# Layer 0's first loads as ordered 256 KB pieces, and VectorE's ids from an on-chip row

## The chip, the core and the metric

The kernel runs on one core of a Trainium2 chip. A core has several engines, each with its own in-order instruction queue: TensorE (PE) multiplies matrices, VectorE (DVE) and ScalarE (ACT) work on rows, GpSimd (POOL) does the same and issues gathers, and SyncE (SP) issues most of the DMA transfers. Sixteen DMA engines move data between DRAM and the on-chip memory of 128 partitions. Products are accumulated in a second on-chip memory, PSUM. The metric is the device time of one launch in microseconds, as the median of several runs.

## What is computed

The input `x` has 64 sequences of 32 positions of 512 numbers. Four residual layers follow one another. Only the first is touched here:

```python
# layer 0: conditioning, then a feed-forward block
w = weight[adapter_ids]                       # 8 sets of 512x512, one chosen per sequence
y = einsum('bsi,boi->bso', x, w)
logits = y @ gate_w                           # 8 experts, top 2
routing, _ = top_k(logits, 2)
h = relu(y @ up_w) ** 2                       # 512 -> 1024
shared = h @ down_w                           # 1024 -> 512
moe = ((y @ fc1_w) @ expert_w) * sum(routing)
routed = moe @ fc2_w
x = x + layernorm(shared + routed) * gamma + beta
```

The ids lie between 3 and 7. Layer 1 is another conditioned feed-forward block, layer 2 is attention over a paged cache with a feed-forward block behind it, and layer 3 is a small last one. All data are float32.

## The kernel before

The 2048 rows of `x` are 16 tiles of 128 rows. A tile holds four sequences (`SEQ = 4`). Layer 0 (`layer0`) works on groups of `G = 4` tiles, so there are four groups, each with 16 sequences and so 16 ids. `KC = 4` is the number of 128-row slices of the inner dimension of 512.

The loads come first, all of them issued by SyncE in the order in which the code names them: the group's transposed input `xT` (1 MB, line 85, which is the line of the helper `load`), the eight `sets` of conditioning weights as one transfer of 2 MB for each slice k (line 159), then `fc1T`, `expert`, the gate columns of `latent`, `up` (2 MB), `down` (2 MB), `fc2`, `gamma` and `beta`.

`products(g, xT)` is a generator which computes y for a group. It first fills 16 VectorE registers with the group's ids (line 171). The source is a row in DRAM:

```python
_, ids = nc.values_load_multi_w_load_instructions(
    a["ids0"][0:1, SEQ * G * g:SEQ * G * (g + 1)], engines=[mybir.EngineType.DVE],
    min_val=0, max_val=n_sets - 1)
```

Then, for each slice k and each tile t, VectorE copies the four chosen 128x512 weight slices, found by register, into a tile `w` (line 179; three such buffers), and TensorE multiplies each sequence's 32 rows by its own slice (line 183), accumulating in PSUM (`py`). That is 64 copies a group. After the last slice each `py` is copied out by VectorE (`y`, line 189), and transposed by TensorE (line 117) with ScalarE copying the result to `yT` (line 118).

For group 0 the generator is run to its end. Then `fc1T` and `expert` are multiplied into `latent` (the product is called `pfe`, line 122). The main loop over groups computes the eight blocks of `h` (`ph`, line 122; relu on ScalarE, line 210; the square as `hT` on VectorE, line 211), and takes two steps of the next group's generator after each block. Then, tile by tile, it computes the routed part (`pl`; `top`, line 221; `routed_by`, line 223; `routed`, line 225), the product with `down` (`pd`, line 228), the transposes of `routed`, the product with `fc2` (line 232) and the normalisation (lines 234 to 245). The last part of the generator (the y copies and transposes of the next group) is taken inside the first tile.

The order on each queue isn't the order of the code: a scheduler places an instruction as soon as it takes its operands to be ready. Nothing in the program before ties a group's register loads to any other work. `tc.issue_after(ins)` is the program's way of saying that what is traced inside it stands behind `ins` on the same engine's queue.

Of the kernel before, what the change touches and what calls it, by code (L numbers as in the profile page):

```python
# [24 lines left out]
F32 = mybir.dt.float32  # L25
I32 = mybir.dt.int32
# [7 lines left out]
P = 128  # L34
B, S, D = 64, 32, 512
NT = B * S // P
SEQ = P // S
KC = D // P
# [90 lines left out]
def layer0(c, x_in, x_out):  # L129

    tc, nc, a = c.tc, c.nc, c.a
    INT, LAT, NE = 1024, 256, 8
    G = 4
    N = G * P
    n_sets = a["cond0T"].shape[0]
    with ExitStack() as ctx:

        fp = ctx.enter_context(tc.tile_pool(name="l0_first", bufs=1))
        sp = ctx.enter_context(tc.tile_pool(name="l0_seq_weights", bufs=3))
        tx = ctx.enter_context(tc.tile_pool(name="l0_transposed_x", bufs=2))
        up_p = ctx.enter_context(tc.tile_pool(name="l0_up", bufs=1))
        wp = ctx.enter_context(tc.tile_pool(name="l0_weights", bufs=1))
        xp = ctx.enter_context(tc.tile_pool(name="l0_x", bufs=2))
        gp = ctx.enter_context(tc.tile_pool(name="l0_group", bufs=2))
        tp = ctx.enter_context(tc.tile_pool(name="l0_tile", bufs=2))
        ps = ctx.enter_context(tc.tile_pool(name="l0_psum", bufs=2, space=PSUM))

        def transposed_x(g):
            return c.load(tx, "xT", [P, KC, N],
                          a["xT"][:, g * N:(g + 1) * N].rearrange("(k p) n -> p k n", p=P))

        xT = transposed_x(0)

        sets = fp.tile([P, KC, n_sets, D], F32, name="sets")
        for k in range(KC):
            nc.sync.dma_start(sets[:, k], a["cond0T"][:, k * P:(k + 1) * P, :].rearrange("e p o -> p e o"))
        fc1T = c.chunks(fp, "fc1T_0")  # L160
        expert = c.chunks(fp, "expert0")
        latent = wp.tile([P, KC, LAT + NE], F32, name="latent")
        nc.sync.dma_start(latent[:, :, LAT:], a["gate0"].rearrange("(k p) n -> p k n", p=P))
        up = c.chunks(up_p, "up0")
        down = c.chunks(wp, "down0")
        fc2 = c.chunks(wp, "fc2_0")
        gamma, beta = c.row(wp, "gamma0"), c.row(wp, "beta0")

        def products(g, xT):

            _, ids = nc.values_load_multi_w_load_instructions(
                a["ids0"][0:1, SEQ * G * g:SEQ * G * (g + 1)], engines=[mybir.EngineType.DVE],
                min_val=0, max_val=n_sets - 1)
            pys = [ps.tile([P, D], F32, tag=f"y{t}", bufs=1, name="py") for t in range(G)]
            for k in range(KC):
                for t in range(G):
                    w = sp.tile([P, SEQ, D], F32, name="w")
                    for j in range(SEQ):
                        nc.vector.tensor_copy(w[:, j, :], sets[:, k, ds(ids[SEQ * t + j], 1), :]
                                              .rearrange("p a o -> p (a o)"))  # L180
                    for j in range(SEQ):
                        q = slice(S * j, S * j + S)
                        nc.tensor.matmul(pys[t][q, :], xT[:, k, t * P + S * j:t * P + S * j + S],  # L183
                                         w[:, j, :], start=k == 0, stop=k == KC - 1)
                    yield
            yT = gp.tile([P, KC, N], F32, name="yT")
            for t in range(G):
                y = tp.tile([P, D], F32, name="y")
                nc.vector.tensor_copy(y, pys[t])
                c.transposed(ps, "tr", y, yT[:, :, t * P:(t + 1) * P])  # L190
            yield yT

        steps = products(0, xT)
        for yT in steps:
            pass
        for m in range(KC):
            pl = ps.tile([P, LAT], F32, tag="tr", name="pfe")
            c.accumulate(pl, [(fc1T[:, k, m * P:(m + 1) * P], expert[:, k, :]) for k in range(LAT // P)])
            nc.scalar.copy(latent[:, m, :LAT], pl)

        for g in range(NT // G):
            more = iter(())
            if g + 1 < NT // G:
                more = products(g + 1, transposed_x(g + 1))
            hT = gp.tile([P, INT // P, N], F32, name="hT", bufs=1)
            for f in range(INT // P):
                ph = ps.tile([P, N], F32, tag="mm", name="ph")
                c.accumulate(ph, [(up[:, k, f * P:(f + 1) * P], yT[:, k, :]) for k in range(KC)])
                r = tp.tile([P, N], F32, name="relu")
                nc.scalar.activation(r, ph, AF.Relu)  # L210
                nc.vector.tensor_tensor(hT[:, f, :], r, ph, ALU.mult)
                for _ in range(2):
                    next(more, None)
            for t in range(G):
                T = G * g + t
                q = slice(t * P, (t + 1) * P)
                xt = c.load(xp, "xt", [P, D], x_in(T))
                pl = ps.tile([P, LAT + NE], F32, tag="tr", name="pl")
                c.accumulate(pl, [(yT[:, k, q], latent[:, k, :]) for k in range(KC)])
                top = tp.tile([P, 8], F32, name="top")  # L220
                nc.vector.max(top, pl[:, LAT:])
                r = tp.tile([P, 1], F32, name="routed_by")
                nc.vector.tensor_tensor(r, top[:, 0:1], top[:, 1:2], ALU.add)
                routed = tp.tile([P, LAT], F32, name="routed")
                nc.scalar.activation(routed, pl[:, :LAT], AF.Copy, scale=r)
                pd = ps.tile([P, D], F32, tag="mm", name="pd")
                for f in range(INT // P):
                    nc.tensor.matmul(pd, hT[:, f, q], down[:, f, :], start=f == 0, stop=False)  # L228
                eT = tp.tile([P, LAT // P, P], F32, name="eT")
                c.transposed(ps, "tr", routed, eT, LAT // P)  # L230
                for m in range(LAT // P):
                    nc.tensor.matmul(pd, eT[:, m, :], fc2[:, m, :], start=False, stop=m == LAT // P - 1)
                stats = tp.tile([P, nc.vector.BN_STATS_DIM], F32, name="stats")
                nc.vector.bn_stats(stats, pd)
                mv = tp.tile([P, nc.vector.BN_AGGR_DIM], F32, name="mv")
                nc.vector.bn_aggr(mv, stats)
                rstd = tp.tile([P, 1], F32, name="rstd")
                nc.vector.tensor_scalar(rstd, mv[:, 1:2], 1e-5, None, ALU.add)
                c.inverse_root(rstd, 1)
                z = tp.tile([P, D], F32, name="z")  # L240
                nc.vector.tensor_scalar(z, pd, mv[:, 0:1], rstd, ALU.subtract, ALU.mult)
                nc.gpsimd.tensor_tensor(z, z, gamma, ALU.mult)
                nc.gpsimd.tensor_tensor(xt, xt, beta, ALU.add)
                nc.vector.tensor_tensor(z, z, xt, ALU.add)
                nc.sync.dma_start(x_out(T), z)
                if t == 0:
                    nxt = next(more, None)
            yT = nxt
# [1060 lines left out]
```

## Time and profile before

| What | Value |
|---|---|
| median of 3 runs | 3705.31 us (3702.78 to 3708.0) |
| profiled execution: its own time | 3732.76 us |
| profiled execution: span, first to last instruction | 3730.8 us |
| granted TensorE clock, mean | 0.995 |
| GpSimd busy | 1261.9 us (34%) |
| DMA over the span | 407.68 MB, mean 109 GB/s |
| DMA queue of SyncE | 251.65 MB |
| largest single group on TensorE | `sc` at line 772, 557.6 us (attention) |
| first TensorE work of the program | at 23.71 us |
| layer 0's last normalisation ends | at some 406 us |

The times of a timeline are microseconds from the start of the span. A row gives the start, the duration, the engine, the line, the operation, the tile written and the tiles read, how many instructions were merged, and in brackets how long the engine was idle before and what ended that. Register operations are not counted as busy time. They show in the chain of waits and in the view of a source line, where an engine's name carries a "q" for its queue (DVEq, SPq).

### The profile page before, as it was taken

The numbers are of one execution on the slowest core, as the hardware profiler recorded it, in microseconds if no ns is written. First come the engines' busy times: TensorE is split into PE (matmuls) and PEld (weight loads), VectorE is DVE, ScalarE is ACT, GpSimd is POOL, SyncE is SP. The second block draws the span as 40 slices with busy tenths as digits, with TensorE's granted clock in tenths as the row PEclk, the third lists the DMA queues.
The fourth block names the chain that finished last, engine by engine and source line by source line (L and its number), as shares of the span: only waits on it lengthen the run. The fifth ranks groups of instructions, "written<-read, shape, count | busy, mean of one in ns | idle before, by whom it ended". The sixth has DMA issues, their size and how long they took to land.

```text
span 3730.8 us, 62064 instructions
## 1 busy us (share of the span) xinstructions
PE 3643.1 (98%) x18752; PEld 2526.2 (68%) x18752; DVE 1807.6 (48%) x4879; ACT 1277.1 (34%) x2950; POOL 1261.9 (34%) x1265
## 2 busy tenths in 40 slices
PE   6999999999999999999999999999999999999899
PEld 3444788888866777677667766677766776677655
DVE  5443222222236555565556555565556655565333
ACT  0111111211124444444444444444444444444311
POOL 0112100000035444544444444444445444444222
PEclk9999999999999999999999999999999999999999
DMA  5104211111044444334443356444444344434321
GB/s 195 34 24 162 99 43 60 43 49 36 32 145 129 123 119 124 115 116 119 121 118 114 117 177 188 153 125 122 122 127 122 118 123 123 123 117 143 119 71 60
DMA packets 408827, 407.68 MB, mean 109 GB/s; under 512 B 49232, under 2 KB 321616, under 8 KB 408496
## 3 DMA queue, kind: packets, MB, share of 16 engines
q1 hardware_dynamic: 361776, 251.65, 22.1%
q0 software_dynamic: 44416, 147.88, 12.8%
q10 hardware_dynamic: 2304, 4.20, 0.3%
q8 instruction: 152, 2.49, 0.3%
q14 instruction: 179, 1.47, 0.1%
HBM read 382.57 MB, written 20.97 MB: 108 GB/s over the span
## 4 chain that ended last, share of the span: by engine, by line
PE 93%; SPq 2%; issue 1%; DVE 1%; another core or an unknown queue 1%; DMA 1%; DVEq 1%; ACT 1%; POOL 0%; ACTq 0%; POOLq 0%
PE po L621 14%; PE sc L772 12%; PE pq L621 11%; PE py L621 11%; PE gate_up L292 10%; PE prT_ps L616 6%; PE pz L292 5%; PE po L1079 3%; PE pk L621 3%; PE ph L122 3%; PE pv L621 3%; PE pd L228 2%; PE po L292 2%; PE qkT_ps L616 2%; PE py L183 1%
## 5 line engine op out<-in xcount | busy, mean ns | idle before, releaser
L643 POOL DMA_INDIRECT vt<-in_v_rows,v_rows x512 | 500.7, 978 | 805.6 <-PE po L621 693.2
L621 PEld LDWEIGHTS po<-prT,vt 128*128 128x128 f32 x4096 | 530.6, 192 | 212.2 <-issue 185.1
L777 DVE CUSTOM_DVE_ANT_0 pr<-sc,mask 128x544 f32<-128x544 f32 x512 | 368.7, 720 | 477.7 <-PE sc L772 394.0
L772 PE MATMUL sc<-kt,qT 128*128 128x288 f32 (+1 forms) x2048 | 557.6, 395 | 12.2 <-DMA kt<-in_kT 8.0
L621 PE MATMUL po<-prT,vt 128*128 128x128 f32 x4096 | 545.3, 276 | 22.1 <-ACT prT L790 18.5
L779 ACT ACTIVATE pr<-pr,low 128x544 f32<-128x544 f32 x512 | 383.6, 749 | 486.7 <-DVE low L777 484.4
L772 PEld LDWEIGHTS sc<-kt,qT 128*128 128x128 f32 x2048 | 369.8, 191 | 189.9 <-issue 83.9
L621 PE MATMUL py<-wo,oT 128*128 128x512 f32 x1024 | 480.5, 593 | 0.8 <-DVE oT L820 0.8
L621 PE MATMUL pq<-wq,xT 128*128 128x512 f32 x1024 | 480.8, 593 | 0.0
L790 ACT COPY prT<-prT_ps 128x512 f32<-128x512 f32 x512 | 298.6, 583 | 441.2 <-PE prT_ps L616 279.6
L784 DVE TENSOR_SCALAR pr<-pr,low 128x512 f32<-128x512 f32 x512 | 324.1, 633 | 16.8
L616 PE MATMUL prT_ps<-ident,pr 128*128 128x128 f32 x2048 | 312.2, 275 | 0.0
L621 PEld LDWEIGHTS py<-wo,oT 128*128 128x128 f32 x1024 | 192.3, 190 | 137.8 <-issue 125.8
L621 PEld LDWEIGHTS pq<-wq,xT 128*128 128x128 f32 x1024 | 182.5, 190 | 130.0 <-issue 125.2
L781 DVE RECIPROCAL low<-low 128x1 f32<-128x1 f32 x512 | 83.4, 163 | 360.0 <-ACT pr L779 321.3
L616 PEld LDWEIGHTS prT_ps<-ident,pr 128*128 128x128 f32 x2048 | 239.0, 142 | 7.6
L126 POOL TENSOR_TENSOR rs<-rs,minus_half 128x4 f32<-128x4 f32 x160 | 166.2, 1039 | 168.3 <-DVE rs L659 166.2
L675 POOL TENSOR_TENSOR rot<-rot,swapped 128x512 f32<-128x512 f32 x160 | 202.6, 1266 | 1.0
L782 ACT ACTIVATE own_pr<-pr,low 128x32 f32<-128x32 f32 x512 | 164.3, 321 | 107.6 <-DVE low L781 104.8
L676 POOL TENSOR_TENSOR rot<-rot,rs 128x512 f32<-128x512 f32 x160 | 181.0, 1132 | 8.0
L376 DVE TENSOR_TENSOR sg<-sg,gate_up 128x256 f32<-128x256 f32 (+1 forms) x88 | 37.0, 420 | 278.4 <-ACT sg L375 278.4
L292 PE MATMUL gate_up<-xT,gate1T 128*128 128x256 f32 (+1 forms) x704 | 168.2, 382 | 0.0
(207 smaller groups left out, 4594.6 us busy)
## 6 DMA issues: line engine op xcount, KB each, us to landing
kt<-in_kT SPq DMA_DIRECT2D x2048, 64.0 KB
xt<-x SPq DMA_DIRECT2D x48, 256.0 KB
wq<-in_WqT SPq DMA_DIRECT2D x12, 1024.0 KB
A<-in_A SPq DMA_DIRECT2D x64, 152.0 KB
sets<-in_cond0T SPq DMA_DIRECT2D x4, 2048.0 KB
vt<-in_v_rows,v_rows POOLq DMA_INDIRECT x512, 3.7
wo<-in_WoT SPq DMA_DIRECT2D x8, 1024.0 KB
y<-y SPq DMA_DIRECT2D x32, 256.0 KB
```

Source lines behind the costliest of these rows:

```text
L126: self.nc.gpsimd.tensor_tensor(t, t, self.minus_half[:, :n], ALU.pow)
L292: c.on_pe(nc.tensor.matmul(out, lhsT, rhs, start=start, stop=stop))
L616: c.on_pe(nc.tensor.transpose(pt[:, m, :], piece, c.ident))
L621: c.on_pe(nc.tensor.matmul(out, lhsT, rhs, start=first and i == 0, stop=last and i == len(pairs) - 1))
L643: nc.gpsimd.indirect_dma_start(out=vts[b % 2][:, n, :], out_offset=None, in_=a["v_rows"], in_offset=bass.IndirectOffsetOnAxis(ap=rows[h][: ...
L675: nc.gpsimd.tensor_tensor(r, r, tmp, ALU.add)
L676: last = nc.gpsimd.tensor_tensor(r, r, rs.unsqueeze(2).to_broadcast([P, REP, HD]), ALU.mult)
L772: c.on_pe(nc.tensor.matmul(sc[:, lo + n * PSIZE:lo + m * PSIZE].rearrange("p (n k) -> p n k", k=PSIZE), q, kt[:, n:m, g, :], start=True, s ...
L777: nc.vector.tensor_tensor_reduce(pr[:, :NK], sc[:, lo:lo + NK], masks[h, b], -SCALE, 3.0e38, ALU.add, ALU.min, low[:, 0:1])
L779: nc.scalar.activation(pr[:, :NK], pr[:, :NK], AF.Exp, bias=low[:, 0:1], scale=-1.0, accum_out=low[:, 1:2])
L784: nc.vector.tensor_scalar(pr[:, :L], pr[:, :L], low[:, 2:3], None, ALU.mult)
L790: nc.scalar.copy(prT, pt)
```

## The change

The ids come on chip once, as a row `numbers` of 64 integers, with a DMA that stands ahead of all others. The register loads read that row. From group 1 on they stand behind the last y copy of the group before (`last_y`), on VectorE's queue.

The first `xT`, the `sets`, `up` and `down` are loaded in pieces of 128x512 numbers (256 KB). The order is slice by slice: the k-th piece of `xT`, then the eight sets' pieces of that slice. `up` follows immediately, its first 512 columns before the others, ahead of `fc1T` and `expert`. Later groups' `xT` are loaded in one transfer as before.

```diff
-        def transposed_x(g):
-            return c.load(tx, "xT", [P, KC, N],
-                          a["xT"][:, g * N:(g + 1) * N].rearrange("(k p) n -> p k n", p=P))
-
-        xT = transposed_x(0)
+        def transposed_x(g, k, xT=None):
+            if k is None:
+                return c.load(tx, "xT", [P, KC, N],
+                              a["xT"][:, g * N:(g + 1) * N].rearrange("(k p) n -> p k n", p=P))
+            nc.sync.dma_start(xT[:, k, :], a["xT"][k * P:(k + 1) * P, g * N:(g + 1) * N])
+
+        def pieces(pool, name):
+            src = a[name]
+            t = pool.tile([P, src.shape[0] // P, src.shape[1]], F32, name=name)
+            for o in range(0, src.shape[1], D):
+                for k in range(src.shape[0] // P):
+                    q = slice(o, min(o + D, src.shape[1]))
+                    nc.sync.dma_start(t[:, k, q], src[k * P:(k + 1) * P, q])
+            return t
+
+        numbers = c.load(fp, "numbers", [1, B], a["ids0"], I32)
+        last_y = []
+        xT = tx.tile([P, KC, N], F32, name="xT")

         sets = fp.tile([P, KC, n_sets, D], F32, name="sets")
         for k in range(KC):
-            nc.sync.dma_start(sets[:, k], a["cond0T"][:, k * P:(k + 1) * P, :].rearrange("e p o -> p e o"))
+            transposed_x(0, k, xT)
+            for e in range(n_sets):
+                nc.sync.dma_start(sets[:, k, e, :], a["cond0T"][e, k * P:(k + 1) * P, :])
+        up = pieces(up_p, "up0")
         fc1T = c.chunks(fp, "fc1T_0")
         expert = c.chunks(fp, "expert0")
...
-        up = c.chunks(up_p, "up0")
-        down = c.chunks(wp, "down0")
+        down = pieces(wp, "down0")
...
         def products(g, xT):

-            _, ids = nc.values_load_multi_w_load_instructions(
-                a["ids0"][0:1, SEQ * G * g:SEQ * G * (g + 1)], engines=[mybir.EngineType.DVE],
-                min_val=0, max_val=n_sets - 1)
+            with tc.issue_after(last_y[0]) if last_y else nullcontext():
+                _, ids = nc.values_load_multi_w_load_instructions(
+                    numbers[0:1, SEQ * G * g:SEQ * G * (g + 1)], engines=[mybir.EngineType.DVE],
+                    min_val=0, max_val=n_sets - 1)
...
-                nc.vector.tensor_copy(y, pys[t])
+                last_y[:] = [nc.vector.tensor_copy(y, pys[t]).ins]
...
-                more = products(g + 1, transposed_x(g + 1))
+                more = products(g + 1, transposed_x(g + 1, None))
```

## The prediction

> **What bounds the kernel.** I read the page first (busy times, chain of waits), then the timeline of the first 125 us by engine, then the chain and the source line of the register loads. The page:
>
> ```profile
> span 3730.8 us, 62064 instructions
> ...
> PE 3643.1 (98%) x18752; PEld 2526.2 (68%) x18752; DVE 1807.6 (48%) x4879; ACT 1277.1 (34%) x2950; POOL 1261.9 (34%) x1265
> ...
> PE 93%; SPq 2%; issue 1%; DVE 1%; another core or an unknown queue 1%; DMA 1%; DVEq 1%; ACT 1%; POOL 0%; ACTq 0%; POOLq 0%
> ```
>
> TensorE sets the end: 98% busy, 93% of the chain. Its idle time is 3730.8 - 3643.1 = 87.7 us, and only what removes some of that, or adds to it, moves the time. The change touches layer 0 alone, so I look where TensorE starts:
>
> ```profile
> 23.71 11.43 PE L183 MATMUL py<-w,xT 128*32 128x512 f32 x64 [23.71 <-DVE w L179]
> 40.52 11.43 PE L183 MATMUL py<-w,xT 128*32 128x512 f32 x64 [5.38 <-DVE w L179]
> 51.88 1.09 PE L117 MATMUL transposed<-ident,y 128*128 128x128 f32 x8
> ...
> 54.72 3.72 PE L122 MATMUL pfe<-expert,fc1T 128*128 128x256 f32 x16
> 58.27 7.03 PE L122 MATMUL ph<-yT,up 128*128 128x512 f32 x16
> 65.23 3.87 PE L183 MATMUL py<-w,xT 128*32 128x512 f32 x32
> ```
>
> Each row is start, duration, work, and in brackets the idle time and what ended it. Two holes, 23.71 and 5.38 us, are ended by VectorE's weight copies; group 0's products end at 40.52 + 11.43 = 51.95. From there TensorE is nearly gapless, so a microsecond won before 51.95 should reach the end. Why are the copies late? VectorE:
>
> ```profile
> 23.23 10.81 DVE L179 COPY w<-sets 128x512 f32 x32 [23.23 <-issue]
> 40.04 10.81 DVE L179 COPY w<-sets 128x512 f32 x32 [5.99 <-issue]
> 50.78 1.27 DVE L189 COPY y<-py 128x512 f32<-128x512 f32 x2
> ```
>
> "issue" means that no engine or DMA is known to have released it. The chain fills these stretches with VectorE's own queue at line 171; that line by itself:
>
> ```profile
> L171 DVEq FUSED_REGOPS  x64: 183/183/203, 8.8 to 62.1; - x64
> L171 DVEq SEQ_ASSERT  x64: 23/23/41, 9.0 to 62.3; - x64
> L171 DVEq TENSOR_LOAD <-in_ids_ptr x4: 930/1316/1648, 0.8 to 54.4; - x4
> L171 DVEq TENSOR_LOAD <-in_ids x4: 1831/2931/7020, 1.7 to 56.1; - x4
> ```
>
> Columns: minimum/median/maximum ns. The chain has a pointer load at 0.76 and a 7.02 us load of ids, 16 pairs of register operations 0.275 us apart (to 13.2), then **a second whole block** from 13.22 (1.65 + 3.24 + 16 pairs) to 23.1, and the last pairs of a third at 35.44 to 39.85. One block serves one group; four groups' loads depend on nothing, so two stand before group 0's first copy and a third in its middle. The holes are registers, not data: the bytes below put set slice k=2 on chip at 23.3, long before 40.04.
>
> **Registers.** Group 0 keeps one block, from an on-chip row. No row has a load from there; its bounds are 0 and 1.83 us (the shortest load from DRAM); I take 1.8. The pointer load goes. The row's own DMA lands about 1.95 us after its issue begins (the small scales load: issued 274.30, consumer at 276.25): 0.74 + 1.95 = 2.7. Then 1.8 + 16 x 0.275 = 6.2: ids ready at 8.9. Blocks 2 and 3 leave the path.
>
> **What is late next: the data.** Windows of 2 us show 12 and 252 GB/s in the first 4 us (0.53 MB) and some 387 GB/s after: as if full rate began at 4.0 - 1.36 = 2.64. The numbers row is issued ahead, 0.43 us by the small loads at 274: 3.1. xT and the sets are 1.05 + 8.39 = 9.44 MB, as before: 24.4 us, to 27.5. From last byte to consumer I take 1.7 us (transfers fade at 46.7, POOL's xt addition starts at 48.40). Slice k=3 is usable at 29.2; its 16 copies take 16 x 0.338 (10.81/32) = 5.4; TensorE ends 1.1 behind VectorE (50.85 against 51.95): **35.7**. Slices arrive each 2.36/0.387 = 6.1 us and cost 5.4 of copies, so earlier slices hide. Slice 0 lands at 3.1 + 6.1 + 1.7 = 10.9, covering the registers by 2.0; without cover they would delay slice 0 alone. Gain: 51.95 - 35.7 = **16.2 us**. The pieces change the arrival of slice 0, not of slice 3, so they bring almost nothing at the end.
>
> **More DMA issues.** 52 pieces (4 xT, 32 sets, 8 up, 8 down) replace 7 issues. A 256 KB issue costs SP about 0.38 + 0.05 us (xt rows), below the 0.68 us that its bytes take, so the queue stays full. [...] The nearest rows are layer 1's 152 KB A pieces, with row gathers beside them:
>
> ```profile
> 300.00:304.00 4.00, 4.00 (x16) 2.48 (x15) 0.49 (x1) 0.37 (x1) 0.81 (x1) 1.00 0.92 261
> ...
> 316.00:320.00 4.00, 4.00 (x11) 1.78 (x10) 0.00 (x0) 0.00 (x0) 0.00 (x0) 1.00 1.05 373
> ```
>
> The last columns are DMA share and GB/s: 261 with an A issue each 0.52 us, 373 when a 256 KB xt follows. Separate transfers overlap here, [...] I take the rows, with 340 GB/s (+3.4 us) as the bad end.
>
> **Order of loads.** up now goes ahead of fc1T and expert. These land after 12.32 MB: 31.8 + 3.1 + 1.7 = 36.6, wanted at 54.72 - 16.2 = 38.5: cover 1.9. The next xT lands after 16.53 MB: 47.5, wanted at 65.23 - 16.2 = 49.0: cover 1.5. down follows before it and is wanted at 103.8 - 16.2. SP's layer-1 register loads (from 52.4) and the third xT (51.98) come later than all issues. If a cover fails, only the excess is lost.
>
> **The blocks behind the copies.** Groups 1, 2, 3 now have a 6.2 us block behind the last y copy (L189) of the group before.
> Group 1: y ends at 53.87 - 16.2 = 37.7, block to 43.9, first w tile (4 copies) 45.2, wanted at 49.0: free. If the first hT (46.3) goes ahead of the block, the tile comes at 54.5: 5.5 lost. I take 0, since the before trace already sends copies out right behind y (53.78).
> Groups 2 and 3: their blocks ran at 31.6 and 54.4, and 12 copies ran ahead at 98.48 to 104.1. Now all wait for the y at 114.17, with routing queued behind them on VectorE:
>
> ```profile
> 114.17 0.67 DVE L189 COPY y<-py 128x512 f32<-128x512 f32 x1
> ...
> 118.68 0.17 DVE L221 MAX8 top<-pl 128x8 f32<-128x8 f32 x1
> ...
> 119.13 0.47 ACT L225 ACTIVATE routed<-pl,routed_by 128x256 f32<-128x256 f32 x1 [2.82 <-DVE routed_by L223]
> ...
> 123.32 0.38 PE L117 MATMUL transposed<-ident,routed 128*128 128x128 f32 x2
> ```
>
> routed is ready at 119.60, TensorE wants it at 123.32: slack 3.7. A block ahead of top costs up to 6.2 - 3.7 = 2.5 a group, one behind it nothing (VectorE idles 7.31 us until 126.35). The copies have until 150. I take 1.0 a group: 2.0.
>
> **Clock.** [...] 0.50 granted from 38 to 44 after the 5.38 us hole. [...] by the row both x64 groups took 11.43 us, VectorE setting the pace, so I add none. The forecast gaps are 6.1 - 5.7 = 0.4 us.
>
> **Sum.** 16.2 - 2.0 = 14.2 us. The profiled execution, 3732.76 us around its 3730.8 us span, becomes some 3718.6. The median is 27 us shorter without the profile, and no row says where; I subtract the difference whole: 3705.3 - 14.2 = **3691**. If register operations are cheaper without profiling, the gain shrinks: at half the time for the 48 pairs in the holes (13.2 us), 6.6 less.
>
> **Rivals.**
> 1. *Blocks in the way* (a wait replaces the removed one): 5.5 + 2.5 + 2.5 = 10.5 lost, net 5.7: 3699.6. For it: all three stand behind a copy on a busy queue. Against: idle rows beside each.
> 2. *Pieces slow the load* (ends slower): the sets land late. Break-even is slice 3 usable at 45.4, that is 9.44 MB in 45.4 - 3.1 - 1.7 = 40.6 us, 232 GB/s; the slope is one for one. [...] The rows (261 and 373) speak against it.
> 3. *More is won*: no block costs anything, lag 0.3 instead of 1.7 (17.6 us), and of the waits behind layer 1's A loads, which SP issues ahead of an xt (3.89 us idle at 325.92), some goes, as the planned order shifts: up to 21.5: 3684. For it: those waits come from the order on SP; against: nothing in the diff touches them.
>
> **Chances.** Forecast 0.72 (3685 to 3697.5), rival 1 and the half-priced registers 0.15, rival 2 0.04, rival 3 0.09. The range 3683 to 3700 holds the forecast, most of rivals 1 and 3, not rival 2. A measurement can tell 0.2%, 7.4 us: below 3697.9 counts as faster. Faster: 0.72 + 0.09 + 0.06 of rival 1: 0.87. Same: 0.09. Slower: 0.04.
>
> **What would show it.** Line 171 once before the first copy, ending near 9; first copy near 11; VectorE idle about 0.7 us between slices on DMA of sets; group 0's products ending at 34 to 37; DMA near 387 GB/s throughout; line 171 after each last y copy, TensorE's wait for routed under 2.5 us. Wrong if products end after 45, DMA falls below 300 GB/s, or TensorE waits over 3 us for w after its first group.

## The result, and the profile after

The changed kernel takes 3690.57 us (median of 7 runs, 3687.09 to 3694.27), the kernel before 3703.56 us beside it. The ratio is 0.9964 with a 95% interval of 0.9954 to 0.9974: 13.3 us less (9.6 to 17.0). Forecast were 3691 and 14.2 us.

The page of the changed kernel, in the lines that were shown of before:

```profile
span 3690.5 us, 62125 instructions
...
PE 3637.0 (99%) x18752; PEld 2523.5 (68%) x18752; DVE 1816.8 (49%) x4879; ACT 1284.4 (35%) x2950; POOL 1259.7 (34%) x1265
```

TensorE's idle time falls from 87.7 to 3690.5 - 3637.0 = 53.5 us. That is more than the timed gain, and an experiment below says why. The start of TensorE's timeline (start, duration, work, idle time before and what ended it):

```profile
11.41 12.38 PE L202 MATMUL py<-w,xT 128*32 128x512 f32 x64 [11.41 <-DVE w L198]
24.24 12.21 PE L202 MATMUL py<-w,xT 128*32 128x512 f32 x64 [0.45 <-DVE w L198]
36.39 1.09 PE L117 MATMUL transposed<-ident,y 128*128 128x128 f32 x8
...
109.37 0.44 PE L117 MATMUL transposed<-ident,routed 128*128 128x128 f32 x2 [1.58 <-ACT routed L244]
...
199.78 0.44 PE L117 MATMUL transposed<-ident,routed 128*128 128x128 f32 x2 [1.94 <-ACT routed L244]
```

The holes of 23.71 and 5.38 us are now 11.41 and 0.45, and group 0's transposes start at 36.39 instead of 51.88: 15.5 us. Two new waits for `routed` stand behind. VectorE shows both sides:

```profile
10.93 5.46 DVE L198 COPY w<-sets 128x512 f32 x16 [10.93 <-DMA xT<-in_xT]
17.23 5.46 DVE L198 COPY w<-sets 128x512 f32 x16 [0.85 <-PE py L202]
23.76 5.46 DVE L198 COPY w<-sets 128x512 f32 x16 [1.07 <-DMA sets<-in_cond0T]
29.90 5.46 DVE L198 COPY w<-sets 128x512 f32 x16 [0.68 <-DMA up<-in_up]
...
101.82 0.17 DVE L240 MAX8 top<-pl 128x8 f32<-128x8 f32 x1 [2.39 <-PE pl L122]
107.53 0.43 DVE L198 COPY w<-sets 128x512 f32 x1 [5.54 <-issue]
107.88 0.80 DVE L260 TENSOR_SCALAR z<-pd,mv,rstd 128x512 f32<-128x512 f32 x1
108.60 0.15 DVE L242 TENSOR_TENSOR routed_by<-top 128x1 f32<-128x1 f32 x1
```

The copies now follow the slices, with gaps of 0.7 to 1.1 us, two of three ended by a transfer. Further down, 5.54 us of "issue" lie between `top` and `routed_by`: the register block of group 2, which in the kernel before ran long ahead of this point. The blocks' rows, by source line (minimum/median/maximum ns):

```profile
L190 DVEq FUSED_REGOPS  x64: 183/183/203, 3.4 to 197.6; - x64
L190 DVEq SEQ_ASSERT  x64: 23/23/41, 3.7 to 197.8; - x64
L190 DVEq TENSOR_LOAD <-numbers x4: 1097/1104/1356, 2.0 to 191.9; - x4
```

The load takes 1.1 us from the row where it took 1.8 to 7.0 from DRAM, and no pointer load stands before it. The register pairs cost the same (medians of 183 and 23 ns in both kernels).

How far the changed kernel is ahead, at the start of the same instruction in the two timelines:

| Point on TensorE | Before | After | Ahead |
|---|---|---|---|
| group 0's transposes of y | 51.88 | 36.39 | 15.5 |
| transpose of `routed`, group 0, tile 0 | 110.69 | 95.00 | 15.7 |
| the same, group 0, tile 1 | 123.32 | 109.37 | 13.9 |
| the same, group 1, tile 1 | 211.57 | 199.78 | 11.8 |
| the same, group 1, tile 2 | 222.16 | 212.11 | 10.1 |
| layer 1's first transpose | 404.31 | 394.73 | 9.6 |

So 5.6 of the 15.7 us are paid back by group 1's third tile. Of these, 3.9 go in two stretches that hold the next group's register block, and 1.7 go behind the second wait, where TensorE's granted clock was 0.50 (202 to 204, last section). From there to layer 1 two things nearly cancel. TensorE waits twice for the normalised `z`, and by the end of these waits the lead has grown to 11.3 us (322.83 against 334.11), since the clock was halved between them in the kernel before (0.50 from 326 to 330) and not in the changed one (1.00 from 312 to 322). Then the clock is halved once more in the changed kernel (0.50 from 324 to 326, 0.78 in the 2 us behind), and the same 56 matmuls take 1.7 us longer (the kernel before, then the changed one):

```profile
334.11 24.30 PE L122 MATMUL ph<-yT,up 128*128 128x512 f32 x56 [0.16 <-DVE z L241]
```

```profile
322.83 26.00 PE L122 MATMUL ph<-yT,up 128*128 128x512 f32 x56 [2.61 <-DVE z L260]
```

### The profile page after: what moved, and what is told of

It reads as the page before. It is cut to its first block, busy times and chain, and to the rows that moved or that the text cites. A ratio compares the mean times of both kernels' runs of the same rounds, so it can differ in the third digit from the quotient of the medians.

```text
span 3690.5 us, 62125 instructions
## 1 busy us (share of the span) xinstructions
PE 3637.0 (99%) x18752; PEld 2523.5 (68%) x18752; DVE 1816.8 (49%) x4879; ACT 1284.4 (35%) x2950; POOL 1259.7 (34%) x1265
## 4 chain that ended last, share of the span: by engine, by line
PE 89%; DMA 1%; SPq 1%; DVE 0%; issue 0%; POOL 0%; ACT 0%; ACTq 0%; POOLq 0%; DVEq 0%
PE po L640 14%; PE sc L791 13%; PE pq L640 12%; PE py L640 12%; PE gate_up L311 10%; PE prT_ps L635 6%; PE pz L311 5%; PE po L1098 3%; PE pv L640 3%; PE pk L640 3%; PE po L311 2%; PE qkT_ps L635 2%; PE pd L247 1%; PE ph L122 1%; PE ph L1098 0%
## 5 line engine op out<-in xcount | busy, mean ns | idle before, releaser
L791 PE MATMUL sc<-kt,qT 128*128 128x288 f32 (+1 forms) x2048 | 557.1, 394 | 11.2 <-DMA kt<-in_kT 6.6
```

The costliest lines, as they stand in the source:

```text
L791: c.on_pe(nc.tensor.matmul(sc[:, lo + n * PSIZE:lo + m * PSIZE].rearrange("p (n k) -> p n k", k=PSIZE), q, kt[:, n:m, g, :], start=True, s ...
```

## The experiments

Line numbers differ between the kernels, since the edits shift them. Ratios are to the kernel before, run beside each.

### Are the pieces or the registers the gain?

`row_and_order` is before with the row and the order, but not the pieces:

```diff
+        numbers = c.load(fp, "numbers", [1, B], a["ids0"], I32)
+        last_y = []
         xT = transposed_x(0)
...
-            _, ids = nc.values_load_multi_w_load_instructions(
-                a["ids0"][0:1, SEQ * G * g:SEQ * G * (g + 1)], engines=[mybir.EngineType.DVE],
-                min_val=0, max_val=n_sets - 1)
+            with tc.issue_after(last_y[0]) if last_y else nullcontext():
+                _, ids = nc.values_load_multi_w_load_instructions(
+                    numbers[0:1, SEQ * G * g:SEQ * G * (g + 1)], engines=[mybir.EngineType.DVE],
+                    min_val=0, max_val=n_sets - 1)
...
-                nc.vector.tensor_copy(y, pys[t])
+                last_y[:] = [nc.vector.tensor_copy(y, pys[t]).ins]
```

> The loads are left as in the kernel before (xT 1 MB, four slices of 2 MB); only the on-chip row and the order behind the y copies are made. Theory A (registers set the gain, slice 3 lands no earlier in pieces): first copy near 13, since slice 0 waits for 3.1 MB, VectorE then never waits long, group 0's products end at 36.5 within 0.7 us as in the changed kernel, layer 1 starts at 394.7 within 1 us, time 3690.6 within 2 us. Theory B (the pieces carry part of it): products end 2 us or more later than 36.45, the time 2 us or more above.

Ratio 0.9966 (0.9952 to 0.998). Its VectorE timeline:

```profile
11.65 10.98 DVE L182 COPY w<-sets 128x512 f32 x32 [11.65 <-DMA sets<-in_cond0T]
23.48 10.88 DVE L182 COPY w<-sets 128x512 f32 x32 [0.85 <-PE py L186]
```

The first copy is 0.7 us later than in the changed kernel, the last one ends earlier: the transposes start at 35.39, 1.0 us before those of the changed kernel. Theory A holds, and the pieces even cost a microsecond here. (In `best` and `pfe_first` below, which differ in the pieces and in where the later blocks stand, it is 1.4.) Layer 1 starts at 391.92, which is 2.8 us earlier and not within 1 us as expected: 1.0 comes from the front, and the other 1.8 is about the 1.7 that the changed kernel's profile lost where its clock was halved the second time. The start of the transfers shows where the microsecond goes, in windows of the changed kernel and then of `row_and_order` (the columns after VectorE's busy time are the granted clock, the DMA share and GB/s):

```profile
2.00:4.00 2.00, 0.00 (x0) 1.00 0.67 115
4.00:6.00 2.00, 0.00 (x0) 1.00 1.00 364
6.00:8.00 2.00, 0.00 (x0) 1.00 0.98 362
...
24.00:28.00 4.00, 4.00 (x13) 1.00 1.05 387
```

```profile
2.00:4.00 2.00, 0.00 (x0) 1.00 0.73 206
4.00:6.00 2.00, 0.00 (x0) 1.00 1.05 409
6.00:8.00 2.00, 0.00 (x0) 1.00 1.05 393
```

The pieces move (206 - 115) x 2 us + (401 - 363) x 4 us = 0.33 MB less in these 6 us, or 0.9 us at 387 GB/s. Why they start slower isn't shown, and the new order of the loads was not tried apart from the pieces.

The converse, `pieces_only`, is the changed kernel with before's register loads:

```diff
-        numbers = c.load(fp, "numbers", [1, B], a["ids0"], I32)
...
-            with tc.issue_after(last_y[0]) if last_y else nullcontext():
-                _, ids = nc.values_load_multi_w_load_instructions(
-                    numbers[0:1, SEQ * G * g:SEQ * G * (g + 1)], engines=[mybir.EngineType.DVE],
-                    min_val=0, max_val=n_sets - 1)
+            _, ids = nc.values_load_multi_w_load_instructions(
+                a["ids0"][0:1, SEQ * G * g:SEQ * G * (g + 1)], engines=[mybir.EngineType.DVE],
+                min_val=0, max_val=n_sets - 1)
```

> The changed kernel's loads; register loads from DRAM and unordered, as before. Theory A: two DRAM blocks before the first copy (near 23), a third before the last 16 copies: VectorE's sum is that of the kernel before, products end at 51.9 within 1.5, time 3703.6 within 2.5: nothing gained. Theory B: first copy near 11 and a gain of over 5 us.

Ratio 1.0007 (0.9998 to 1.0015): nothing gained. The timeline of VectorE, though, isn't what was expected:

```profile
23.45 16.19 DVE L196 COPY w<-sets 128x512 f32 x48 [23.45 <-DMA sets<-in_cond0T]
50.61 6.29 DVE L196 COPY w<-sets 128x512 f32 x16 [10.97 <-DMA xt<-in_x]
```

The third block, 5.99 us of idle time in the kernel before, is 10.97 us here, and the products' transposes start at 58.90, not 51.9. That is 7 us later, while the timed median is only 2.6 us above the kernel before, so this one profile seems to show more than the usual run loses. The block's load of ids took 6.68 us here and 2.62 in the kernel before. Over the runs, such loads from DRAM take 1.8 us where the DMA engines are quiet (`order_only` at 108.9 and 200.9, DMA share 0.00 beside them) and 2.5 to 8.3 us at the start or beside full traffic. Traffic thus goes with long loads. Why one load under full traffic took 2.62 us and another 6.68 stays open.

### The row or the order?

`order_only` keeps the loads from DRAM (and has no row), `row_only` leaves the blocks unordered. Against `row_and_order`:

```diff
 order_only:
-                    numbers[0:1, SEQ * G * g:SEQ * G * (g + 1)], engines=[mybir.EngineType.DVE],
+                    a["ids0"][0:1, SEQ * G * g:SEQ * G * (g + 1)], engines=[mybir.EngineType.DVE],
 row_only:
-            with tc.issue_after(last_y[0]) if last_y else nullcontext():
-                _, ids = nc.values_load_multi_w_load_instructions(
...
+            _, ids = nc.values_load_multi_w_load_instructions(
```

> Before's loads and register loads from DRAM; only the order (the next group's block behind this group's y copies). Theory A: one block in front: 0.76 + 0.93 + 7.0 + 4.4, first copy near 13.2, products end near 36.5: the order alone brings nearly all of the 15.5 us at that point. But each later block has its pointer load and DRAM load (1.3 + 2 instead of 1.1), so the two blocks between top and routed_by are 2 us longer: layer 1 starts at 394.7 + 4 = 398.7; time near 3694.5. Theory C (the on-chip row is needed): products end after 41.

> Before's loads; the row on chip, no order. Theory A: two blocks of 5.5 us in front of the copies and one before the last 16: first copy at 13, VectorE busy or in registers through 2.0 + 3 x 5.5 + 64 x 0.341 = 40.3, products end at 41.4, some 5 us later than in the changed kernel; the blocks of groups 2 and 3 then no longer hold up routing, which gives 5.6 us back: layer 1 starts near 394.5 to 395.5, the time is 3691 within 3. Theory C (the row matters more than the order): products end at 36.5, layer 1 starts near 389.5.

`order_only`: ratio 0.9992 (0.9984 to 1.0001). The front is near what was expected: first copy at 14.84, transposes at 37.43, each 1 to 2 us late (its first load took 8.3 us). What was won there is lost behind. TensorE's waits in the first 420 us (total, times, longest):

```profile
PE py L185 <- DVE w L181: 15.3, 1, 15.3
PE transposed L117 <- ACT routed L227: 7.2, 2, 3.9
PE ph L122 <- DVE z L243: 4.4, 2, 2.6
PE ph L122 <- DVE hT L213: 3.3, 1, 3.3
```

The waits for `routed` double from 3.5 us to 7.2, and group 1's block, now 7.79 us of idle time on VectorE, holds up a first `hT` as well (3.3). Two of these waits are followed by a halved clock (0.50 at 54 to 56 and at 212 to 214). I had expected 3694.5 and had not counted group 1; it came to 3701.4.

`row_only`: ratio 0.9957 (0.994 to 0.9973), as fast as the changed kernel. Its three blocks in front of and between the copies are short:

```profile
14.05 16.19 DVE L181 COPY w<-sets 128x512 f32 x48 [14.05 <-issue]
33.93 5.46 DVE L181 COPY w<-sets 128x512 f32 x16 [3.69 <-issue]
```

Its products end 4 us later than in the changed kernel (transposes at 40.57), but it waits nowhere for `routed`. Its lead over the kernel before is 11.2 us at the first `routed` transpose (99.49 against 110.69) and still 11.2 at the last of layer 0 (310.44 against 321.64), where the changed kernel's has fallen from 15.7 to 10.0. Layer 1 starts at 393.45. Theory A is right in its parts: **the row alone brings the gain**. The order takes the other groups' blocks off the front and puts two of them where they cost about as much.

### Do the later blocks cost what the table says?

`behind_routing` moves the blocks of groups 2 and 3 into VectorE's longest idle stretch:

```diff
-        last_y = []
+        last_y, first_routed = [], []
...
-            with tc.issue_after(last_y[0]) if last_y else nullcontext():
+            behind = first_routed or last_y
+            with tc.issue_after(behind[0]) if behind else nullcontext():
...
-                nc.vector.tensor_tensor(r, top[:, 0:1], top[:, 1:2], ALU.add)
+                routed_by = nc.vector.tensor_tensor(r, top[:, 0:1], top[:, 1:2], ALU.add).ins
+                if t == 0:
+                    first_routed[:] = [routed_by]
```

> The changed kernel, but the blocks of groups 2 and 3 stand behind the first tile's routed_by of the loop before the one that uses them, where VectorE is idle for 7.15 us until a transpose ends (88.70 to 95.85), instead of behind the last y copy. If the blocks between top and routed_by cost the 5.65 us that layer 0 loses between its 1st and its 7th routed transposes (15.7 ahead of before falling to 10.05), that loss goes: routed transposes at 95.0, 107.7, 118.3 and then 15.7 ahead to the end of layer 0, layer 1 starts near 389.1, time near 3685. If they cost nothing (rival: the stall has another cause, such as the 12 w copies ahead), layer 1 starts at 394.7, time 3690.6.

The wait for `routed` is gone, but only part of the loss is. From group 0's first `routed` transpose to its second TensorE takes 13.59 us, against 12.63 in the kernel before and 14.37 in the changed one. Timed, nothing is gained: ratio 0.9966 (0.9955 to 0.9977), with layer 1 at 392.06 and not at 389.1. VectorE's timeline:

```profile
89.67 0.16 DVE L243 TENSOR_TENSOR routed_by<-top 128x1 f32<-128x1 f32 x1
95.40 3.45 DVE L199 COPY w<-sets 128x512 f32 x10 [5.57 <-issue]
98.76 0.69 DVE L209 COPY y<-py 128x512 f32<-128x512 f32 x1
```

The block sits in the idle stretch, but it frees ten weight copies, and these go ahead of the y copy: the rival named there had a part in it. `routing_clear` therefore queues the first copies too, and was run beside the changed kernel (`after_again`):

```diff
+            behind, ahead = first_routed or last_y, list(last_y)
...
-                    for j in range(SEQ):
-                        nc.vector.tensor_copy(w[:, j, :], sets[:, k, ds(ids[SEQ * t + j], 1), :]
-                                              .rearrange("p a o -> p (a o)"))
+                    with tc.issue_after(ahead[0]) if ahead and k == 0 and t < 3 else nullcontext():
+                        for j in range(SEQ):
+                            nc.vector.tensor_copy(w[:, j, :], sets[:, k, ds(ids[SEQ * t + j], 1), :]
+                                                  .rearrange("p a o -> p (a o)"))
```

Here `ahead` is the last y copy of the group before. The other edits are those of `behind_routing`.

> The changed kernel once more, on the chip of the two kernels that follow, to compare them with. Expected: ratio to before 0.9964 within its interval, layer 1 starting at 394.7 within 1 us, the two waits of the routed transposes again 1.5 to 2 us each.

> As behind_routing, and the first 12 w copies of the next group are queued behind the last y copy, since in behind_routing ten of them ran ahead of a y copy (95.40 to 98.85) and held up a transpose. If the blocks and these copies are all that layer 0 loses behind its products: no wait for routed, y at its old place, 15.5 us ahead of before until the 13th routed transposes, layer 1 starts 5.0 to 5.7 us earlier than in after_again, ratio 0.0015 lower (0.995). If w copies now hold up top or routed_by: a wait of up to 1 us for routed returns in each of two groups.

`after_again`: ratio 0.9962 (0.995 to 0.9975). The waits for `routed` are again 1.59 and 1.93 us, but layer 1 starts at 391.99, 2.7 us before the 394.7 that was expected. Neither of the two stretches of halved clock that cost the first profile 1.7 us each is there (it has one at 314 to 318 instead, and the wait behind it is shorter: 0.92 us, not 2.61). `routing_clear`: 0.995 (0.9938 to 0.9962), layer 1 at 386.72, so 5.3 us earlier, and no wait for `routed`. The two intervals overlap, so it is the profiles that tell them apart. The lead of `routing_clear` over the first profile of the kernel before is 15.8 us at the first `routed` transpose (94.91) and 15.8 at the last (305.86), while that of `after_again` falls from 15.4 to 11.4. The placement of the blocks, with the copies that they set free, was the loss.

### A better version

`pfe_first` is `behind_routing` with the small product's loads and work in front; `best` is `routing_clear` with the same edit and without the pieces:

```diff
         numbers = c.load(fp, "numbers", [1, B], a["ids0"], I32)
+        fc1T = c.chunks(fp, "fc1T_0")
+        expert = c.chunks(fp, "expert0")
...
+        for m in range(KC):
+            pl = ps.tile([P, LAT], F32, tag="tr", name="pfe")
...
         steps = products(0, xT)
```

> behind_routing, and besides fc1T and expert are loaded ahead of the sets and multiplied (pfe) before group 0's products. If the landing of slice 3 sets the end of the products: they end 0.79 MB / 0.387 = 2.0 us later (38.5), and the 3.7 us of pfe leave the path: 1.7 us better, layer 1 near 387.4, time near 3683.3. If VectorE or something else sets it: products end at 36.5 and the gain is 3.7.

> routing_clear with the loads of the kernel before (no pieces), and pfe with its loads first. By row_and_order the products end 1.0 us earlier without pieces, by pfe_first the loads cost 2.0 to 2.8 and the 3.7 us of pfe leave the path: 1.9 to 2.7 us ahead of routing_clear at the start of layer 1, that is 7 to 8.4 ahead of after_again; ratio to before near 0.9944.

`pfe_first`: transposes at 38.92, 2.8 us later than in `behind_routing` (36.11; 2.0 were expected), and layer 1 at 390.01, 2.0 us earlier. So the landing of slice 3 does set the end of the products. Ratio 0.9955; its interval (0.994 to 0.9969) overlaps with that of `behind_routing`. `best`: ratio 0.9943 (0.993 to 0.9956), which beats the kernel before clearly, and the changed one beside it (0.9962) by about 0.002, with intervals that just overlap. In the profile layer 1 starts at 386.23, only 0.5 us before `routing_clear`, not 2 to 2.7: it lies 1.4 us ahead until 305, and loses part in the waits behind. That `best` is faster than `routing_clear` isn't shown.

### How small may a piece be?

`small_pieces` cuts the changed kernel's sets by partitions, so that the rows stay at 2 KB:

```diff
             for e in range(n_sets):
-                nc.sync.dma_start(sets[:, k, e, :], a["cond0T"][e, k * P:(k + 1) * P, :])
+                for r in range(0, P, 32):
+                    nc.sync.dma_start(sets[r:r + 32, k, e, :], a["cond0T"][e, k * P + r:k * P + r + 32, :])
```

> The changed kernel with the sets in pieces of 32 partitions, 64 KB, rows of 2 KB as before: 128 issues instead of 32. If SP's issue interval decides (0.33 + 0.08 us, by the 64 KB kt rows): 133 issues end at 0.74 + 133 x 0.41 = 55, slice 3 usable near 57, products end near 63.5, 27 later than 36.45; time near 3717. If bytes decide: 36.5 and 3690.6. [...]

Ratio 1.0088 (1.0071 to 1.0105), transposes at 73.33. SP's own queue:

```profile
1.59 14.80 SPq L178 DMA_DIRECT2D sets<-in_cond0T  x32
16.43 0.42 SPq L155 DMA_DIRECT2D xT<-in_xT  x1
16.90 14.97 SPq L178 DMA_DIRECT2D sets<-in_cond0T  x32
```

32 issues take 14.80 us, 0.46 each, and 64 KB in that time are 142 GB/s. The DMA engines are busy for 0.54 of the time from 4 to 60 us (1.04 in the changed kernel from 4 to 24), and SP issues without a gap over 0.1 us. So SP's issue interval decides, somewhat longer than expected, hence 73 rather than 63.5. At 256 KB the changed kernel's first eight issues for the sets take 3.98 us, 0.50 each, less than the 0.68 us which the bytes take at 387 GB/s. Pieces of 64 KB over all 128 partitions were not tried.

### Why the two profiles differ by 40 us

> The kernel before, profiled once more. Its first profile spans 3730.8 us while its timed median is 3703.6; layer 0 explains 9.6 of the 40.3 us between the two profiles. If the rest belongs to that one execution: a span near 3700, sixteenths of attention of 151.7 us as in the changed kernel (152.3 in the first), products end again at 51.9. If it belongs to the kernel: span near 3731 again.

The span is 3719.5 us, in a series in which the kernel before has a median of 3720.5. So the level differs between series, and an absolute time is compared only within one. The products' transposes start at 54.07, not at 51.9: the loads of ids took longer, the first 7.98 us instead of 7.02. Layer 1 starts at 405.02, close to the first profile's 404.31. The extra time lies behind that, most of it in attention, whose instructions stand in the same order in both kernels on every engine. TensorE's waits from 420 us on (total, times, longest), first in this run, then the two longest in the profile of the changed kernel:

```profile
PE po L621 <- ACT prT L790: 12.1, 7, 3.3
```

```profile
PE sc L791 <- DMA kt<-in_kT: 6.6, 3, 3.9
PE sc L791 <- ACT qT L748: 2.4, 3, 1.0
```

The first profile of before has 18.5 us of the first of these waits (the product `po` for ScalarE's copy `prT`), `after_again` 12.2, the changed kernel's profile 0.2. It comes and goes with the run, not with the change. In the five profiles other than that first one whose series have a median near 3704 for the kernel before it is 0.2 us; in the seven of the series near 3720 and 3725 it is 8.2 to 14.8, with the change and without. What sets it is open. Of the 40.3 us between the two spans the change explains 9.6. The other 30.7 lie behind the start of layer 1, and 18.3 of them are this wait.

## Why the prediction was right

**What bounds.** Right: the hole at the start was register loads, and what was won there went on to TensorE's later work.

**Registers.** Right, a little dear: 1.8 us was taken for the load from the row, and it took 1.36 at the start and 1.10 later. The ids were ready near 3.4 + 16 x 0.275 = 7.8 (8.9 forecast), and the data hid them.

**The data.** The first copy came at 10.93 (10.9 forecast), gaps between slices 0.7 to 1.1 (0.7), the products' end at 36.45 (35.7). The term was 16.2 us. It measured 15.5 in the first pair of profiles and 54.07 - 36.26 = 17.8 in the second, since the loads from DRAM in the kernel before differ. What was missing is the slow start of the pieces, 1.0 us by `row_and_order`.

**The pieces.** "Almost nothing at the end" was right; they cost that microsecond. The 387 GB/s that were taken from the rows held at 256 KB (24 to 28). At 64 KB pieces did cost, by the issue interval of 0.46 us.

**Blocks behind the copies.** Right for group 1, whose first tile came well before it was wanted. For groups 2 and 3 the mechanism was as described (a block in front of the routing, a slack of 3.7 us), only the size was off: 1.0 us a group was taken, the waits were 1.58 and 1.94, within the bound of 2.5, and the second was followed by a granted clock of 0.50, which cost 1.7 us. In all 2.0 were forecast against 5.6, or 3.9 without the clock. It was the mis-sized term of the sum. That a halved clock could follow a wait for `routed` wasn't considered: the paragraph on the clock looked at the gaps between slices alone.

**The sum.** 14.2 were forecast. Timed it is 13.3 and, in the later series, a ratio of 0.9962. At the start of layer 1 the first pair of profiles gives 9.6 us and the second 405.02 - 391.99 = 13.0. The changed kernel's first profile holds two stretches of halved clock, 1.7 us each, that its second doesn't have. So the mechanism was right, but that the forecast came within a microsecond of the timed gain is in part luck. In the first pair the front gave 0.7 us less and the blocks, without the clock, cost 1.9 more than was taken, and the stretch with the waits near 313 to 334, which the sum leaves out, gave 1.2 back. In the second pair a front of 17.8 made up for the blocks. That the row alone would have done as well wasn't foreseen: the prediction summed the edits, and didn't ask what each is worth without the others.

## What to carry to other kernels

Register loads that depended on nothing stood at the front of VectorE's queue here and held the first copy back to 23.23 us; look for "issue" ahead of the first work, and put their source on chip before thinking of order. A block pinned behind some instruction also stands ahead of others (here 5.54 us ahead of `routed_by`): count what is queued behind it, and what it sets free. When loads and compute are cut finer, ask what the last piece's landing does, not the first's, and whether the issuing queue keeps up (0.46 us an issue was too slow at 64 KB).

## What was not expected of the hardware

Behind a gap of 1.94 us the granted TensorE clock was 0.50 in one run of the changed kernel, and behind one of 1.93 us it stayed at 1.00 in another. Windows behind the second wait of the first profile (the columns after TensorE's busy time are the granted clock, the DMA share and GB/s), then of `after_again`:

```profile
200.00:202.00 2.00, 2.00 (x7) 0.64 0.00 0
202.00:204.00 2.00, 2.00 (x4) 0.50 0.68 248
204.00:206.00 2.00, 2.00 (x8) 1.00 0.04 14
```

```profile
200.00:202.00 2.00, 1.91 (x8) 1.00 0.00 0
202.00:204.00 2.00, 2.00 (x8) 1.00 0.59 214
```

In the first, four matmuls of `pd` took 3.22 us instead of 1.88, and the kernel lost 1.7 us more than the wait itself.

The length of the gap alone doesn't decide it. In `order_only` the clock stayed at 1.00 behind a gap of 3.31 us:

```profile
117.14 0.44 PE L117 MATMUL transposed<-ident,routed 128*128 128x128 f32 x2 [3.31 <-ACT routed L227]
```

```profile
116.00:118.00 2.00, 0.86 (x5) 1.00 0.00 0
118.00:120.00 2.00, 2.00 (x7) 1.00 0.13 50
```

In the changed kernel's first profile the clock stayed at 1.00 behind 1.58 us (108 to 114) and 2.82 us (314 to 322) as well, while it was 0.50 behind 2.61 us (324 to 326). In the kernel before the clock fell within the hole of 5.38 us and not only behind it: TensorE was idle from 35.14 to 40.52, and the clock was 0.50 from 38 to 44. What decides, beside the length of the gap, no run here shows. A forecast can only carry it as a risk: in the first profile of the changed kernel it cost 1.7 us twice.
